# Two bottleneck blocks on one core: the step from the first 1x1 convolution into the 3x3 one, with ScalarE's order written out, idle matmuls moved, and a product split around another

## The chip, the cores and the metric

One core of one Trainium2 chip. The metric is the device time of one execution in microseconds; times in the profile are from the start of the profiled span. Engines are named as the profile names them: PE is TensorE's matmuls, PEld its weight loads, DVE is VectorE, ACT is ScalarE, POOL is GpSimd, SP is SyncE, which issues most transfers.

## What is computed

```python
def block(x, w1, b1, g1, be1, w2, b2, g2, be2, w3, b3, g3, be3, residual_scale):
    out = relu(bn(conv1x1(x, w1) + b1, g1, be1))        # 1024 -> 256 channels
    out = relu(bn(conv3x3(out, w2, pad=1) + b2, g2, be2))
    out = bn(conv1x1(out, w3) + b3, g3, be3)            # 256 -> 1024 channels
    return relu(x + softplus(residual_scale)[0] * out)

x = block(x, *first_weights)       # x: 64 x 1024 x 14 x 14, float32
x = block(x, *second_weights)
```

`bn` normalises each channel by the mean and the variance of the whole batch, so a convolution has to be finished before its result can be normalised.

## The kernel before

**Stages.** Block one's first 1x1 convolution runs by itself (up to about 305 us). Its 3x3 convolution follows (to 584 us), then statistics of the third convolution by way of a Gram matrix, then a fused stage in which block one's last convolution and block two's first one alternate (to 1259 us), then block two's 3x3 convolution (to 1541 us), its Gram matrix and its last convolution. The activations between the convolutions, 256 channels in two halves ("slots"), stay in SBUF as `y`.

**The 1x1 convolutions** are block products with 7 instead of 8 products (class `Seven`). Product k is the method `pk`; each of the first convolution's has CS // 2 = 4 matmuls on one PSUM bank, and the methods are generators that yield after each matmul. p6, p7 and p4 add to the same bank `y`; after p7, `after7` has ScalarE copy that bank out (`saved`), before p4 adds to it. The last tiles of images go through `Conv1.closing`, which writes the order of the products out: p1, p4 of the tiles before, p6, p5, p7, p4, then `border.affine_of(1)` and `border.norm(1)` (scale, shift and normalisation of slot 1), and the rest. `late` is true in block one, where a tile pair has 392 columns a matmul, and false in block two, where it has 196.

**The 3x3 convolution** (`conv2`) is Winograd-like. Rows go in six linear combinations per group of 8 images (8 groups, NG), made by VectorE: the pairs (1, 2), (3, 4) and (5, 0). For each combination i VectorE makes `r`, and from it `sums`, `diffs` and `v` (differences of neighbouring columns); ScalarE fills in the two edge columns of `v` (lines 682 and 683). TensorE makes products: `m` from `sums`, `l` from `diffs`, and `columns` from `v`, added to a bank pair on which ScalarE has first put `m` (`put`, lines 835 and 837). ScalarE copies `l` to `ls` (`middle`, lines 849 and 851), and VectorE adds `columns` and `ls` to `f` (line 870), from which the rows of the result are put together in `finish`. Bank pairs `columns`, banks `l` and banks `m` are double.

**The border.** The first pair of combinations is made slot by slot (`first_combination`), slot 1 ahead, begun within `closing` by `border.steps`. Its two products, `first` and `second`, are done in parts by slot: the loop over `s` at the end of `conv2`. In that loop `first` adds `m` straight to its bank pair, and between two steps two matmuls of 448 columns by the identity run on `second.banks`; what they leave there is overwritten by `second.put`. After the loop, the products follow each other in a fixed pattern: `item.middle`, `item.columns(EVEN)`, the next product's `start` (its `m` and `put`), `item.columns(ODD)`, `finished.send(item)`.

**What sets the order.** A scheduling layer orders each engine's instructions. Those that go through `tc.keep_in_program_order` (all matmuls by the helper at line 175, ScalarE's by the helper `act` at line 338, VectorE's by `run`) keep the program's order on their engine; the others are placed by the layer. So a bare `nc.scalar.activation` may come before or after its neighbours in the program.

Of the kernel before, what the change touches and what calls it, by code (L numbers as in the profile page):

```python
# [42 lines left out]
P = 128  # L43
# [47 lines left out]
def bottlenecks(ctx: ExitStack, tc: tile.TileContext, x, w1s, w2s, w3s, pars, out):  # L91
# [248 lines left out]
    class Conv1(Seven):  # L340
# [41 lines left out]
        def closing(self, before):  # L382

            border = self.border
            late = len(self.ts) > 1

            def summary(s):
                summarize(self.stats[:, s : s + 1], T // 2 - 1, T - len(self.ts), PX)  # L390

            yield from self.p1()
            yield from before.p4()
            summary(1)
            if not late:
                yield from before.p3()
                summary(0)
            yield from self.p6()
            yield from self.p5()
            yield from self.p7()  # L400
            yield from self.p4()
            border.affine_of(1)
            border.norm(1)
            if late:
                yield from before.p3()
                summary(0)
            border.begin()
            if late:
                border.steps(1)
            yield from self.p2()  # L410
            if late:
                border.steps(2)
            yield from self.p3()
            border.affine_of(0, lambda: border.steps(1 if late else 3))
            border.norm(0)
            border.steps(5 if late else 6)
# [181 lines left out]
    def conv2(b, par, aff, early, rest):  # L598
# [50 lines left out]
        class Inputs:  # L649

            def __init__(self, pair, run=lambda ins: None):
                self.pair, self.run = pair, run
                self.tiles = tiles = full if pair[0] == 3 else RT
                self.lines = lines = tiles * GI
                n = len(pair) * MS * lines

                def part(tag, width):
                    v = place(tag, 2 * MS * RT * GI * width)  # L660
                    return v[:, : n * width].rearrange("p (k s l c) -> p k s l c", k=2, s=MS, c=width)

                self.r, self.v = part("r", W), part("v", W)
                self.sums, self.diffs = part("sums", WH), part("diffs", WH)
# [8 lines left out]
            def step_columns(self, k=slice(0, 2), s=both):  # L673
# [8 lines left out]
                nc.scalar.activation(v[:, :, :, :, 0], r[:, :, :, :, 0], AF.Copy)  # L682
                nc.scalar.activation(v[:, :, :, :, W - 1], r[:, :, :, :, W - 1], AF.Copy, scale=-1.0)

            def subtract_columns(self, k=slice(0, 2), s=both):
                r = self.r[:, k, s]
# [26 lines left out]
        def first_combination(x, s, t):  # L713

            run, here = x.run, slice(s, s + 1)
            ra, rb = (x.rows(k)[:, s] for k in range(2))
            t = t.rearrange("p (r l) -> p r l", r=RT)
            t2, t1 = t[:, :, :LINE], t[:, :, LINE:]  # L720
            act(t[:, RT - 1], y_all[:, s, GPX - 2 * LINE : GPX], AF.Copy, scale=-3.0)
            run(stt(t[:, :full], two_rows(0, s)[:, :, 0], -4.0, two_rows(0, s)[:, :, 1]))
            yield
            run(nc.vector.tensor_add(ra, t1, t2))
            yield
            x.add_columns(slice(0, 1), here)
            yield
            first, second = x.subtract_columns, x.step_columns
            if s == 0:
                first, second = second, first  # L730
            first(slice(0, 1), here)
            yield
            second(slice(0, 1), here)
            yield
            run(nc.vector.tensor_sub(rb, t1, t2))
            yield
            x.add_columns(slice(1, 2), here)
            yield
            x.subtract_columns(slice(1, 2), here)
            yield  # L740
            x.step_columns(slice(1, 2), here)
            yield

        def combine(g, pair):
            x = Inputs(pair)
            ra, rb = (x.rows(k) for k in range(2))

            if pair[0] == 1:
# [39 lines left out]
        class Products:  # L788
# [39 lines left out]
            def put(self, m):  # L828

                if True:  # L830
                    for q in (EVEN, ODD):
                        v = self.banks[:, q]
                        if self.i == 1:
                            for o in range(MS):
                                nc.scalar.activation(v[:, o], m[:, o], AF.Identity, bias=par[:, B2 + o : B2 + o + 1])
                        else:
                            nc.scalar.activation(v, m, AF.Copy)  # L837

            def middle(self, l=None):

                if l is None:
                    l = self.whole("l", DIFF, self.diffs)
# [2 lines left out]
                for q, sign in (EVEN, 1.0), (ODD, -1.0):  # L845
                    if self.first:
                        for o in range(MS):
                            bias = par[:, B2 + o : B2 + o + 1]
                            nc.scalar.activation(self.ls[:, q, o], l[:, o], AF.Identity, bias=bias, scale=sign)
                    else:  # L850
                        nc.scalar.activation(self.ls[:, q], l, AF.Copy, scale=sign)

            def columns(self, *qs, slots=range(MS), sums=None):
                steps = {ODD: (D3M1, self.r[:, :, :, WH:]), EVEN: (D0M2, self.r[:, :, :, :WH])}
# [171 lines left out]

        inputs = Inputs(order[0], tc.keep_in_program_order)
        t = early.tile([P, RT * 2 * LINE], FP, tag="fa", name="t")  # L1030
        yield from first_combination(inputs, 1, t)
        psum, pool, stats = rest
# [7 lines left out]
            pass  # L1040
        coming, finished = items(), finish()
        next(finished)
        queue.append(next(coming))

        both_columns = EVEN, ODD
        first.open()
        second.open()
        l, m, l2 = first.bank("l"), second.bank("m"), second.bank("l")
        for s in reversed(range(MS)):
            first.columns(*both_columns, slots=[s], sums=True)  # L1050
            if s:
# [658 lines left out]
```

## Time and profile before

| | |
|---|---|
| median of 3 runs | 1929.17 us (1928.47 to 1929.77) |
| profiled execution | 1928.93 us |
| its span | 1927.2 us |
| TensorE (PE) busy | 1905.0 us |
| VectorE (DVE) busy | 1547.5 us |
| ScalarE (ACT) busy | 1085.5 us |
| mean granted TensorE clock | 0.997 of full speed |

A row of the timeline has the start, the length, the engine, the line of the source, the operation, the tiles (output, arrow, inputs), shapes and the number of instructions merged into the row; the brackets hold the engine's idle time before the row and what ended it. A matmul of four-byte numbers stands as two records, so four matmuls are "x8". The ends of matmuls are modelled, some 0.16 us later than the start of the next one in a running stream. A row of waits has the sum in microseconds, the count and the longest one.

### The profile page before, as it was taken

What the parts mean: (1) busy time and instruction counts of PE and PEld (TensorE: products, weight loads), DVE (VectorE), ACT (ScalarE), POOL (GpSimd) and SP (SyncE); (2) the same over time, 40 slices, a digit from 0 to 9 for tenths busy, and PEclk for the clock granted to TensorE, in tenths of its full rate; (3) what the DMA queues carried; (4) which work ended last, traced back from release to release, by engine and by line L of the source; (5) the groups of instructions that cost most, each with busy time, mean ns of one, the idle gap of its engine ahead of it and who ended that gap; (6) DMA issues with size and microseconds to landing.
All of it is one profiled execution on the core that took longest, in us unless ns stands there. A gap on an engine that the chain in (4) does not pass through costs nothing.

```text
span 1927.2 us, 28719 instructions
## 1 busy us (share of the span) xinstructions
PE 1905.0 (99%) x10232; PEld 1600.9 (83%) x10232; DVE 1547.5 (80%) x2509; ACT 1085.5 (56%) x2152; POOL 565.2 (29%) x678
## 2 busy tenths in 40 slices
PE   9999998999999999999999999989999999999999
PEld 5555557999998899999999999989999986555555
DVE  5788767999998866676767767789999986888886
ACT  2222214677778355555555555546777682666666
POOL 0111100211204143433434334302121041666664
PEclk9999999999999999999999999999999999999999
DMA  7777634797856544444444444348879466889998
GB/s 287 273 249 276 220 148 134 202 228 207 213 180 169 190 162 169 168 171 180 179 173 168 167 180 179 123 151 208 221 207 224 141 170 236 291 326 348 329 336 301
DMA packets 198527, 408.77 MB, mean 212 GB/s; under 512 B 37104, under 2 KB 175024, under 8 KB 181872
## 3 DMA queue, kind: packets, MB, share of 16 engines
q1 hardware_dynamic: 159712, 321.85, 49.0%
q0 software_dynamic: 33056, 34.03, 8.5%
q10 hardware_dynamic: 5616, 51.06, 6.4%
q8 instruction: 81, 1.33, 0.3%
q14 instruction: 62, 0.51, 0.1%
HBM read 263.75 MB, written 115.34 MB: 197 GB/s over the span
## 4 chain that ended last, share of the span: by engine, by line
PE 95%; DVE 2%; DMA 1%; ACT 1%; issue 1%; POOL 0%; SPq 0%; DVEq 0%; ACTq 0%; POOLq 0%
PE ay L175 18%; PE cy L175 17%; PE columns L175 14%; PE cp L175 12%; PE ap L175 10%; PE m L175 7%; PE l L175 7%; PE cx L175 5%; PE ax L175 5%; PE ps L175 1%; DMA x<-mid 0%; DMA home<-y 0%; DMA x<-in_x 0%; POOL home L1160 0%; DVE v L677 0%
## 5 line engine op out<-in xcount | busy, mean ns | idle before, releaser
L338 ACT ACTIVATE cu<-cy,scale 128x196 f32<-128x196 f32 (+1 forms) x552 | 256.7, 474 | 278.4 <-PE cy L175 273.2
L175 PE MATMUL columns<-v,ub 128*128 128x224 f32 (+1 forms) x1536 | 303.7, 339 | 5.7 <-ACT columns L837 5.7
L338 ACT ACTIVATE x<-x,shift 128x392 f32<-128x392 f32 x452 | 255.0, 613 | 72.6 <-POOL x L534 53.5
L175 PEld LDWEIGHTS columns<-v,ub 128*128 128x128 f32 x1536 | 270.0, 189 | 11.1 <-ACT columns L837 6.4
L508 DVE SCALAR_TENSOR_TENSOR x<-cp,scale,x 128x196 f32<-128x196 f32 (+1 forms) x368 | 177.8, 483 | 98.6 <-PE cp L175 96.9
L175 PE MATMUL cy<-ct,ws 128*128 128x196 f32 (+1 forms) x736 | 221.8, 383 | 1.2 <-ACT cu L338 1.2
L175 PE MATMUL ay<-at,ws 128*128 128x196 f32 (+1 forms) x768 | 212.7, 382 | 0.0
L529 POOL TENSOR_TENSOR x<-x,cu 128x196 f32<-128x196 f32 (+1 forms) x184 | 159.8, 869 | 171.9 <-ACT cu L338 163.9
L534 POOL TENSOR_TENSOR x<-x,cu 128x392 f32<-128x392 f32 x124 | 125.9, 1016 | 191.4 <-DVE x L508 191.4
L175 PEld LDWEIGHTS ay<-at,ws 128*128 128x128 f32 x768 | 139.3, 190 | 34.5
L175 PEld LDWEIGHTS cy<-ct,ws 128*128 128x128 f32 x736 | 133.4, 190 | 36.4 <-ACT cu L338 4.2
L175 PE MATMUL l<-diffs,ub 128*128 128x224 f32 (+1 forms) x768 | 150.4, 338 | 1.0 <-PE columns L175 0.6
L555 POOL TENSOR_TENSOR x<-x,cu 128x392 f32<-128x392 f32 x120 | 121.9, 1017 | 86.3 <-DVE x L508 81.5
L175 PE MATMUL m<-sums,ua 128*128 128x224 f32 (+1 forms) x752 | 146.3, 337 | 0.2 <-DVE sums L671 0.2
L338 ACT ACTIVATE au<-ay 128x196 f32<-128x196 f32 (+1 forms) x140 | 53.5, 382 | 150.8 <-PE ay L175 148.1
L175 PEld LDWEIGHTS l<-diffs,ub 128*128 128x128 f32 x768 | 134.9, 190 | 2.9 <-PE columns L175 1.2
L508 DVE SCALAR_TENSOR_TENSOR x<-cx,scale,x 128x196 f32<-128x196 f32 (+1 forms) x184 | 89.0, 484 | 56.8 <-PE cx L175 56.8
L175 PEld LDWEIGHTS m<-sums,ua 128*128 128x128 f32 x752 | 132.1, 190 | 1.2 <-DVE sums L671 0.5
L175 PE MATMUL cy<-y,w 128*128 128x196 f32 (+1 forms) x408 | 125.3, 393 | 0.0
L175 PE MATMUL cx<-y,w 128*128 128x196 f32 (+1 forms) x400 | 122.6, 391 | 0.0
L837 ACT ACTIVATE columns<-m 128x448 f32<-128x448 f32 (+1 forms) x160 | 78.6, 491 | 70.5 <-PE m L175 68.3
L175 PE MATMUL cp<-y,ws 128*128 128x196 f32 (+1 forms) x368 | 113.6, 390 | 0.6 <-DVE x L508 0.6
(234 smaller groups left out, 3949.6 us busy)
## 6 DMA issues: line engine op xcount, KB each, us to landing
x<-in_x SPq DMA_DIRECT2D x62, 1568.0 KB, 7.0
ub<-u SPq DMA_DIRECT2D x92, 768.0 KB, 5.7
x<-mid SPq DMA_DIRECT2D x32, 1568.0 KB, 8.3
mid<-x ACTq DMA_DIRECT2D x31, 1568.0 KB, 5.1
out<-x SPq DMA_DIRECT2D x123, 392.0 KB, 5.2
ua<-u SPq DMA_DIRECT2D x92, 256.0 KB, 3.3
u<-y POOLq DMA_DIRECT2D x48, 256.0 KB, 5.7
home<-y SPq DMA_DIRECT2D x70, 96.0 KB, 3.6
```

Of the source, the lines that this page charges most:

```text
L175: tc.keep_in_program_order(nc.tensor.matmul(*args, **kw))
L338: tc.keep_in_program_order(nc.scalar.activation(*args, **kw))
L508: nc.vector.scalar_tensor_tensor(v, bank, self.scale[:, o : o + 1], v, ALU.mult, ALU.add)
L529: nc.gpsimd.tensor_add(self.part(1, 1), self.part(1, 1), u3)
L534: nc.gpsimd.tensor_add(v, v, self.u12)
L555: nc.gpsimd.tensor_add(v, v, self.u12[:, i * self.n : (i + 1) * self.n])
L837: nc.scalar.activation(v, m, AF.Copy)
```

## The change

- `closing`: two of the four matmuls of another product (p3 of the tiles before in block one, p2 in block two) are issued between p7 and p4; the other two follow `border.norm(1)`.
- `Inputs`: the two edge copies of ScalarE become a method, `step_edges`. `first_combination` calls it right after the first row sum, ahead of VectorE's other steps (in both slots). They and the edge copies of pair (3, 4) of group 0 are issued by `act`, in the program's order.
- The border loop: `second.put` and `second.middle` and the bias form of `middle` are issued by `act`; `second.middle` moves up to the end of the loop, ahead of `finished.send(first)`. The next pair's combination, `next(coming)`, moves from before the loop to after `second.middle`.
- Idle matmuls: `fill`. In block one they stay where they were (two). In block two four are issued ahead of the loop, and none in it.

In the order of instructions that the scheduling layer makes of it, TensorE changes by these alone, and GpSimd's and SyncE's queues keep their order. On ScalarE, around the border, the two edge copies of pair (3, 4) move from before the first `ls` (block one) or from between the bank copies (block two) to after the second product's `ls`; in block two the third product's bank copies then come ahead of the four row copies into `r`, in block one they stay behind them. On VectorE, block one is the same up to the second group's combination, where an `f` moves ahead of `sums` and `diffs` moves behind the writes of `y`, just ahead of the next `steps`; in block two `f` of the first product moves ahead of `sums` of pair (3, 4), `f` of the second ahead of the second step into `r`, and a few later ones change places up to the second group.

```diff
@@ closing
             yield from self.p7()
+
+            between = before.p3() if late else self.p2()
+            yield from itertools.islice(between, CS // 4)
             yield from self.p4()
             border.affine_of(1)
             border.norm(1)
+            yield from between
             if late:
-                yield from before.p3()
                 summary(0)
             border.begin()
             if late:
                 border.steps(1)
-            yield from self.p2()
+                yield from self.p2()
...
@@ Inputs
-            def __init__(self, pair, run=lambda ins: None):
-                self.pair, self.run = pair, run
+            def __init__(self, pair, run=lambda ins: None, copy=nc.scalar.activation):
+                self.pair, self.run, self.copy = pair, run, copy
...
+            def step_edges(self, k=slice(0, 2), s=both):
+
+                r, v = self.r[:, k, s], self.v[:, k, s]
+                self.copy(v[:, :, :, :, 0], r[:, :, :, :, 0], AF.Copy)
+                self.copy(v[:, :, :, :, W - 1], r[:, :, :, :, W - 1], AF.Copy, scale=-1.0)
+
+            def step_columns(self, k=slice(0, 2), s=both, edges=True):
+                if edges:
+                    self.step_edges(k, s)
...
@@ first_combination
             run(nc.vector.tensor_add(ra, t1, t2))
+            x.step_edges(slice(0, 1), here)
             yield
             x.add_columns(slice(0, 1), here)
             yield
-            first, second = x.subtract_columns, x.step_columns
+            first, second = x.subtract_columns, partial(x.step_columns, edges=False)
...
@@ combine
-            x = Inputs(pair)
+            x = Inputs(pair, copy=act if g == 0 and pair[0] == 3 else nc.scalar.activation)
...
@@ Products
+            def fill(self, times=1):
+
+                n = MS * self.n
+                for q in (EVEN, ODD) * times:
+                    v = self.banks[:, q].rearrange("p o n -> p (o n)")
+                    matmul(v, ident, ident[:, :1].to_broadcast([P, n]), start=True, stop=True)
+
+            def put(self, m, copy=nc.scalar.activation):
...
-                            nc.scalar.activation(v, m, AF.Copy)
+                        copy(v, m, AF.Copy)
...
-                            nc.scalar.activation(self.ls[:, q, o], l[:, o], AF.Identity, bias=bias, scale=sign)
+                            act(self.ls[:, q, o], l[:, o], AF.Identity, bias=bias, scale=sign)
                     else:
-                        nc.scalar.activation(self.ls[:, q], l, AF.Copy, scale=sign)
+                        copy(self.ls[:, q], l, AF.Copy, scale=sign)
...
@@ the border at the end of conv2
-        inputs = Inputs(order[0], tc.keep_in_program_order)
+        inputs = Inputs(order[0], tc.keep_in_program_order, act)
...
-        queue.append(next(coming))
...
         l, m, l2 = first.bank("l"), second.bank("m"), second.bank("l")
+        if b == 1:
+            second.fill(2)
         for s in reversed(range(MS)):
             first.columns(*both_columns, slots=[s], sums=True)
             if s:
                 first.part(l, DIFF, first.diffs, s)
-                n = MS * second.n
-                for q in both_columns:
-                    v = second.banks[:, q].rearrange("p o n -> p (o n)")
-                    matmul(v, ident, ident[:, :1].to_broadcast([P, n]), start=True, stop=True)
+                if b == 0:
+                    second.fill()
             first.columns(*both_columns, slots=[s])
             if s == 0:
                 first.part(l, DIFF, first.diffs, s)
                 first.middle(l)
             second.part(m, SUM, second.sums, s)
             if s == 0:
-                second.put(m)
-                long_work(0, 0)
-                finished.send(first)
+                second.put(m, act)
             second.part(l2, DIFF, second.diffs, s)
+        second.middle(l2, act)
+        queue += list(itertools.islice(coming, 1))
+        long_work(0, 0)
+        finished.send(first)
         queue = queue[1:] + list(itertools.islice(coming, 1))
         for k in range(1, NG * NF):
             item, more = queue[0], queue[1:2]
             qs = both_columns
-            item.middle(l2 if k == 1 else None)
+            if k > 1:
+                item.middle()
```

More of the change, by code (lines that the diff above doesn't have):

```diff
@@ L671, in add_columns @@
                 self.run(nc.vector.tensor_add(self.sums[:, k, s], r[:, :, :, :, WH:], r[:, :, :, :, :WH]))
-            def step_columns(self, k=slice(0, 2), s=both):
+            def step_edges(self, k=slice(0, 2), s=both):
[5 more added lines that the diff above has]
+                    self.step_edges(k, s)
                 r, v = self.r[:, k, s], self.v[:, k, s]
@@ L681, in step_columns @@
                 )
-                nc.scalar.activation(v[:, :, :, :, 0], r[:, :, :, :, 0], AF.Copy)
-                nc.scalar.activation(v[:, :, :, :, W - 1], r[:, :, :, :, W - 1], AF.Copy, scale=-1.0)
             def subtract_columns(self, k=slice(0, 2), s=both):
@@ L826, in open, with middle @@
                 self.banks = columns()[:, :, : MS * self.n].rearrange("p q (o n) -> p q o n", o=MS)
[L828 to L839, printed above, removed]
+            def fill(self, times=1):
[4 more added lines that the diff above has]
+            def put(self, m, copy=nc.scalar.activation):
+                for q in (EVEN, ODD):
+                    v = self.banks[:, q]
+                    if self.i == 1:
+                        for o in range(MS):
+                            nc.scalar.activation(v[:, o], m[:, o], AF.Identity, bias=par[:, B2 + o : B2 + o + 1])
+                    else:
+                        copy(v, m, AF.Copy)
+            def middle(self, l=None, copy=nc.scalar.activation):
                 if l is None:
```

## The prediction

> **What bounds the kernel now.** I read the page's engine totals first, then who waited for whom on TensorE, then the stretches around the longest waits, then the timelines of TensorE, ScalarE and VectorE there.
>
> ```profile
> PE 1905.0 (99%) x10232; PEld 1600.9 (83%) x10232; DVE 1547.5 (80%) x2509; ACT 1085.5 (56%) x2152; POOL 565.2 (29%) x678
> ...
> PE columns L175 <- ACT columns L837: 5.7, 2, 4.5
> PE columns L175 <- issue: 3.8, 1, 3.8
> ...
> PE ay L175 <- ACT au L338: 1.0, 2, 0.6
> ```
>
> TensorE is the bound: its waits come to some 17 us, and the first two lines (sum, count, longest) hold 9.5 of them. All three lines lie at the two borders, about 287 to 330 us (block one) and 1250 to 1290 us (block two). Columns of the next view: stretch, length, busy time and count of PE, weight loads, DVE, ACT and POOL, granted clock, DMA share, GB/s.
>
> ```profile
> 320.00:325.00 5.00, 2.48 (x7) 2.28 (x8) 4.66 (x6) 4.34 (x12) 0.00 (x0) 0.78 0.30 100
> 1260.00:1265.00 5.00, 1.77 (x5) 1.66 (x6) 4.66 (x16) 2.96 (x6) 0.15 (x2) 0.65 0.86 263
> 1265.00:1270.00 5.00, 5.00 (x16) 3.85 (x15) 4.79 (x11) 1.94 (x8) 0.00 (x0) 0.67 0.33 122
> ```
>
> The long waits are paid twice: the clock is below 1 after them. TensorE's timeline, block one and then two:
>
> ```profile
> 317.12 0.92 PE L175 MATMUL l<-diffs,ub 128*128 128x224 f32 x4
> 322.52 3.09 PE L175 MATMUL columns<-v,ub 128*128 128x224 f32 x8 [4.48 <-ACT columns L837]
> ...
> 1263.23 3.33 PE L175 MATMUL columns<-sums,ua 128*128 128x224 f32 x8 [3.81 <-issue]
> 1266.35 1.70 PE L175 MATMUL l<-diffs,ub 128*128 128x224 f32 x4
> 1267.84 1.92 PE L175 MATMUL columns<-ident 128*128 128x448 f32 x4
> 1269.59 1.70 PE L175 MATMUL columns<-v,ub 128*128 128x224 f32 x8
> ...
> 1279.33 1.81 PE L175 MATMUL columns<-v,ub 128*128 128x224 f32 x8 [1.19 <-ACT columns L837]
> ```
>
> Eight records of 224 columns take 3.1 us after either long wait, and 1.55 elsewhere. What held ScalarE in block one:
>
> ```profile
> 319.16 0.37 ACT L682 ACTIVATE v<-r 128x96 f32<-128x96 f32 x1 [5.39 <-DVE r L640]
> 319.44 0.35 ACT L683 ACTIVATE v<-r 128x96 f32<-128x96 f32 x1
> 319.69 1.45 ACT L849 ACTIVATE ls<-l,par 128x224 f32<-128x224 f32 x4
> ...
> 321.90 0.57 ACT L837 ACTIVATE columns<-m 128x448 f32<-128x448 f32 x1
> ```
>
> The edge copies of the next pair stood first in ScalarE's order and waited 5.39 us for VectorE, while l had been ready since 316.5; the bank copy that TensorE needs came last.
>
> [...] waits of 4.48 and 3.81 us are followed by half rate, the one of 1.19 us is not. [...] That is the third wait above: product four adds to the bank that ScalarE is copying out (0.59 us at 294.17, 0.42 at 1255.17).
>
> **Part one, two matmuls ahead of product four.** A product takes 2.63 us in block one (eight records), so two of its four matmuls take 1.32. Without its wait product four could start at 293.42 (294.17 less 0.59, less the 0.16 of modelled tail). It will start at 293.42+1.32=294.74, not at 294.17; the row after a wait costs 0.1 more (2.73 from start to start), which is saved, so it ends 0.47 late. On it hang, one after the other, y, its statistics, the scale, the norm, VectorE's first sums (304.44) and the first columns (304.89): 0.47 late, with TensorE idle from about 304.1, some 1.5 us. The next wait, for diffs at 307.15, hangs on VectorE's step at 305.00, which today waits 0.17 for TensorE; so from there on 0.3 late. In block two the half product takes 0.665: 1254.59+0.67=1255.26 against 1255.17, and the saved 0.1 cancels it: nothing lost. TensorE is through with the convolution at 1258.6 instead of 1259.3. Split product and whole one write the same results; nothing else moves on VectorE, and the DMA queues keep their order. The weight loads that wait for the freed activations start no later.
>
> **Part two, idle matmuls in block two.** Two of 448 columns took 1.52 us at full clock (307.98 to 309.50); four take 3.04, from 1258.6 to 1261.6. They write a bank whose users are already done; the one wait before them is on TensorE itself. VectorE's sums (1262.73+0.39) are unmoved, so TensorE then idles 1.6 us, well under the 3.81 that halved the clock. I take full clock: first columns 1.51 instead of 3.12, l 0.76 instead of 1.49, the two old idle matmuls (1.75) gone: 4.1 us. The next v is ready at 1264.74, before it is needed at 1265.5, and later inputs are just in time (sums 1268.39, needed 1268.55). Below: none if the clock is half all the same (bounds of this part, 1.75 and 4.1).
>
> **Part three, ScalarE's order.** In the new order the four ls, the two bank copies and the next two ls come first, the edge copies after.
> Block one: l is out at 316.53+0.3; four ls 1.33, two bank copies 1.03, hand-over 0.1: TensorE goes on at 319.3, not 322.52: 3.2. The wait shrinks to 1.1, so the half rate (4.44 us for 2.68 of work) goes too: 1.8. Sum 5.0. What is late next: the third product's bank copies stand behind four row copies (1.41 us) that wait for VectorE's diffs, which now end at 319.5 plus sums 0.78, v 1.27, f 1.00, diffs 0.85, 323.4. So 323.4+1.41+0.90=325.7, while TensorE has reached it at 324.7: 1.0 back. Those columns begin at 325.7 instead of 329.64: **3.9**.
> Block two: l out at 1272.5, plus 1.33 and 1.03: TensorE at 1275.0 instead of 1279.33, 4.3. Then f is ahead of sums on VectorE (1.0 us): sums end at 1277.3 while TensorE is there at 1276.6. The third m begins at 1277.3, not 1280.97: **3.7**.
>
> **What VectorE gives back.** It is busy 33 of 34 us in each group of the convolution (32.8 to 33.7 in windows of 34), so it cannot follow freely. Block two: from the second product's f (1283.26 was the start of that run, with no idle until the diffs end at 1305.68) 22.4 us of work remain; f can now start at 1280.2, when TensorE has the second columns out, so diffs end at 1302.6 and TensorE's l starts 3.1 early instead of 3.7. **Block two: 3.1.**
> Block one: VectorE advances only 1.4 (its idle at 328.70). In its new order diffs stand after the five writes of y, just before the step at 348.31: they end at 348.31-1.4=346.9, and TensorE comes at 350.29-3.9=346.4: 0.5 lost, 0.6 with the restart. In the next group ScalarE's copy of fa (400.01) stands between the two bank copies, and TensorE had 0.7 to spare there (400.74 to 401.46). With TensorE 3.2 and VectorE 1.8 ahead, 0.7 is lost; I put 0.8 for that group. **Block one: 3.9-0.6-0.8=2.5.** Later groups keep their order, and TensorE's lead over VectorE is used up.
>
> **The sum.** 3.1+2.5=5.6 us. What follows the convolutions waits on TensorE's and VectorE's last products, including the loads of x, so it moves along. The profiled execution took 1928.93 us (span 1927.2, 1.7 around it): 1923.3. It is 0.24 under the median of 1929.17, so as a median **1923.6 us**.
>
> **Rivals.**
> - VectorE takes all that it can: TensorE keeps 1.4 and 3.1, 4.5: 1924.7. For it: 0.3 to 1.0 us of idle per group. Against: TensorE reads most of its operands over 3 us after they are made (sums 354.96 for m at 359.44).
> - Nothing is given back: 3.9+3.7=7.6: 1921.6. It needs VectorE's diffs earlier than its order has them.
> - The clock still halves, in the 1.5 and 1.6 us waits ahead of the first columns. Price as in the rows: 1.8 and 2.3. At one border 1925.5 or so, at both 1927.7. Against: 1.19 us left it alone.
> - Slower: VectorE becomes the bound of both convolutions. ScalarE serves TensorE's copies earlier and its row copies for VectorE later (VectorE waits 0.6 for them once a group), VectorE loses that again in each group, and its slack is gone. At twice the wait, 0.6 more in 14 groups is 8.4: 1932.0 after the gain of 5.6. It decides from 0.4 a group. Against: from the second group on the order is the old one.
> - That the change misses its mark: the idle matmuls could wait for the readers of the old bank (until 1260.0); then they end at 1263.1 and part two is the same.
>
> **Numbers.** Forecast 0.57 (its own range 1922.3 to 1924.6), VectorE takes all 0.20, nothing given back 0.10, clock 0.10, slower 0.03. Range 1921.2 to 1925.8: the outer gains, less or more than the spread of the runs (0.7), and the clock at one border. About 0.2%, 3.9 us, is what a measurement can tell from no change: faster by more than that means under 1925.3, the forecast, the third case and most of the first rival: 0.80; same 0.17; slower 0.03.
>
> **What would show it.** Clock 1.00 in both borders; TensorE on second columns near 319.3 and 1275.0 with waits of about 1.1; four idle matmuls ahead of the first columns of block two; first columns of block one about 0.5 late; waits of TensorE on l behind diffs near 347 and 1302.6. It is wrong if the clock falls, if TensorE waits for VectorE in every group, or if a wait behind the row copies at 325 is over 2 us.

## The result, and the profile after

The changed kernel takes **1924.15 us** (median of 11 runs, 1922.67 to 1927.3); the kernel before took 1928.66 us in its 11 runs of the same session (1927.42 to 1930.24). The ratio is 0.9975, with a 95% interval of 0.9965 to 0.9984: 3.1 to 6.8 us less. The profiled execution took 1924.15 us, its span 1922.4 us, 4.8 less than before. The forecast was 1923.6 us.

The page's engine line and TensorE's waits (sum, times, longest) after the change:

```profile
PE 1903.6 (99%) x10236; PEld 1598.7 (83%) x10236; DVE 1547.8 (81%) x2509; ACT 1085.1 (56%) x2152; POOL 566.0 (29%) x678
```

```profile
PE columns L175 <- ACT columns L338: 2.1, 2, 1.0
PE l L175 <- PE columns L175: 1.8, 3, 0.8
...
PE columns L175 <- issue: 1.5, 1, 1.5
...
PE columns L175 <- DVE sums L674: 1.2, 1, 1.2
```

The waits of 4.5 and 3.8 us are gone, and so are the two of product four on ScalarE's copy of its bank. In their place stand several of about 1 us; those on `l` (second line) and on `sums` (last line) are behind VectorE. The view puts the waits on `l` down to PE, but in the timelines the `l` of the second group starts 0.1 us after VectorE's `diffs` has ended, in both blocks. TensorE has four matmul records more than before, the two more idle matmuls, and is busy 1.4 us less: the half rate is gone. The stretches at the borders, columns as before:

```profile
320.00:325.00 5.00, 4.63 (x29) 4.32 (x27) 4.60 (x5) 2.23 (x8) 0.00 (x0) 1.00 0.50 148
1260.00:1265.00 5.00, 4.05 (x21) 4.04 (x22) 4.79 (x14) 2.68 (x6) 0.00 (x0) 1.00 0.76 259
1265.00:1270.00 5.00, 5.00 (x28) 4.94 (x28) 4.86 (x9) 0.82 (x4) 0.00 (x0) 1.00 0.12 34
```

The granted clock (third number from the end) is 1.00 where it was 0.78, 0.65 and 0.67. TensorE's timeline, first block one, then block two:

```profile
305.08 1.78 PE L175 MATMUL columns<-sums,ua 128*128 128x224 f32 x8 [1.25 <-DVE sums L674]
...
319.00 1.81 PE L175 MATMUL columns<-v,ub 128*128 128x224 f32 x8 [1.03 <-ACT columns L338]
...
325.36 1.42 PE L175 MATMUL columns<-v,ub 128*128 128x168 f32 x8 [0.72 <-ACT columns L853]
...
346.88 1.75 PE L175 MATMUL l<-diffs,ub 128*128 128x224 f32 x8 [0.62 <-PE columns L175]
...
1256.31 3.18 PE L175 MATMUL columns<-ident 128*128 128x448 f32 x8
1260.95 1.75 PE L175 MATMUL columns<-sums,ua 128*128 128x224 f32 x8 [1.46 <-issue]
...
1272.88 1.81 PE L175 MATMUL columns<-v,ub 128*128 128x224 f32 x8 [1.04 <-ACT columns L338]
...
1300.56 1.75 PE L175 MATMUL l<-diffs,ub 128*128 128x224 f32 x8 [0.78 <-PE columns L175]
```

What released ScalarE, in block one:

```profile
316.50 1.46 ACT L338 ACTIVATE ls<-l,par 128x224 f32<-128x224 f32 x4 [2.79 <-PE l L175]
317.83 1.12 ACT L338 ACTIVATE columns<-m 128x448 f32<-128x448 f32 x2
318.87 0.97 ACT L338 ACTIVATE ls<-l 128x448 f32<-128x448 f32 x2
319.71 0.64 ACT L338 ACTIVATE v<-r 128x96 f32<-128x96 f32 x2
323.09 0.39 ACT L640 ACTIVATE r<-y 128x224 f32<-128x224 f32 x1 [2.74 <-DVE diffs L696]
```

Now the `ls` wait for TensorE's `l` and start with it, the bank copies follow, and the edge copies stand behind.

**Where the time came from.** I compare stretches, not the whole span. Block one's stretch runs from the start of product six (the row `ay<-at,ws` at 285.52 before, 285.23 after) to the first matmul `m<-ident` behind the convolution. Block two's runs from the row `ap<-x,ws` near 1249, where TensorE waits 0.3 us for `y`, to the first `m<-ident` behind its convolution. Block one takes 298.55 us before and 296.22 after, block two 291.51 and 288.60: 2.33 and 2.91 us less. These two lengths are the better measure: block two takes 288.58 to 288.60 us in the changed kernel and in the four runs below that leave its idle matmuls there and VectorE's order in block two alone, and block one takes 296.22 us both here and in the run that leaves it untouched. The rest of the program is not so steady: over all fourteen profiles the part ahead of block one's stretch takes 285.1 to 286.7 us, the part between the two 665.0 to 666.2, and the part behind 384.5 to 387.7, in no order that follows an edit.

TensorE's lead over the kernel before, from the start of each row in both timelines (0.29 us, by which the changed kernel's profile entered block one earlier, taken off; in block two 2.28):

| TensorE starts | before | after | lead | forecast |
|---|---|---|---|---|
| block one, first columns | 304.89 | 305.08 | -0.5 | -0.47 |
| l behind diffs | 307.15 | 307.09 | -0.2 | -0.3 |
| second columns | 322.52 | 319.00 | 3.2 | 3.2 |
| l, after the half clock | 328.50 | 323.33 | 4.9 | 5.0 |
| third columns | 329.64 | 325.36 | 4.0 | 3.9 |
| l of the second group | 350.29 | 346.88 | 3.1 | 3.3 |
| end of the stretch | 584.07 | 581.46 | 2.3 | 2.5 |
| block two, first columns | 1263.23 | 1260.95 | 0.0 | 0 |
| next v | 1269.59 | 1263.30 | 4.0 | 4.1 |
| second columns | 1279.33 | 1272.88 | 4.2 | 4.3 |
| l of the second group | 1305.77 | 1300.56 | 2.9 | 3.1 |
| end of the stretch | 1540.71 | 1535.52 | 2.9 | 3.1 |

### The profile page after: what moved, and what is told of

Read it like the earlier page. It is cut to its first block, busy times and chain, and to the rows that moved or that the text cites. A ratio compares the mean times of both kernels' runs of the same rounds, so it can differ in the third digit from the quotient of the medians.

```text
span 1922.4 us, 28731 instructions
## 1 busy us (share of the span) xinstructions
PE 1903.6 (99%) x10236; PEld 1598.7 (83%) x10236; DVE 1547.8 (81%) x2509; ACT 1085.1 (56%) x2152; POOL 566.0 (29%) x678
## 4 chain that ended last, share of the span: by engine, by line
PE 93%; DVE 4%; DMA 2%; issue 1%; ACT 1%; POOL 0%; SPq 0%; DVEq 0%; ACTq 0%; POOLq 0%
PE ay L175 17%; PE cy L175 17%; PE columns L175 13%; PE cp L175 11%; PE ap L175 10%; PE m L175 7%; PE l L175 6%; PE cx L175 5%; PE ax L175 4%; PE ps L175 1%; DMA x<-mid 1%; DMA home<-y 1%; DVE v L688 0%; DMA out<-x 0%; DVE steps L773 0%
## 5 line engine op out<-in xcount | busy, mean ns | idle before, releaser
L175 PE MATMUL cy<-ct,w 128*128 128x196 f32 (+1 forms) x368 | 110.9, 383 | 0.5 <-ACT cu L338 0.5
```

The costliest lines, as they stand in the source:

```text
L175: tc.keep_in_program_order(nc.tensor.matmul(*args, **kw))
```

## The experiments

**Theory.** Block one's gain is ScalarE's order, block two's the idle matmuls, which leave the loop and take the place of idleness ahead of the first columns; the split costs a little. TensorE is then ahead of VectorE by more than VectorE's order allows, and what is over is waited for at `l`. **Rivals:** the split brings part of the gain; a wait taken from TensorE is kept in full; the row copies on ScalarE, not VectorE, are what comes next.

All lengths below are of the two stretches; "before" for the times is the kernel before in the same session, 1929.23 us for the first four; 1928.82 for the one with the bank copies first and the one without idle matmuls; 1929.15 for the other four.

The scheduling layer answers some of these edits by moving instructions of VectorE and ScalarE too. By the profiles, both engines keep the order of the kernel that was edited, instruction by instruction, in the run without the split, in block one of the run with ScalarE's order alone, and in every block that an edit leaves untouched. Where they do not, the text says so.

### One part alone, three times

The split alone, on the kernel before:

```diff
             yield from self.p7()
+            between = before.p3() if late else self.p2()
+            yield from itertools.islice(between, CS // 4)
             yield from self.p4()
...
+            yield from between
```

> The kernel before with the split product alone. Measured as the time from the start of p6 in the closing order to the first filler matmul behind the 3x3 convolution: 298.55 us in block one before and 296.23 in the changed kernel; in block two, from the first p6 matmul after its short wait, 291.51 and 288.60. Theory (the gain is ScalarE's order in block one and the idle matmuls in block two; the split puts product four later and so costs): block one 0.2 to 0.4 slower than before, the 4.5 us wait and the half clock still there. Rival (the split gives what it covers, 0.6 and 0.4): block one 0.6 faster. Block two is not clean: the scheduling layer places ScalarE's and VectorE's steps there differently from before, so up to 2 us faster may come of that alone.

1926.83 us, ratio 0.9988 (0.998 to 0.9996). Block one 299.61, block two 290.20. Block one has the new wait of 1.25 us and keeps the old one of 4.48. It is 1.06 us longer than in the first profile of the kernel before, more than expected; the last two runs show that the clock accounts for all but 0.20 of it. In block two the wait ahead of the first columns is 4.48 instead of 3.81, as the half product is through earlier, and the half rate follows it (3.32 us for the eight records of these columns, 1.75 in the changed kernel); yet the stretch is 1.3 us shorter, and the later waits at `m` and `l` are gone. The run isn't clean there: with this edit the scheduling layer also put VectorE's and ScalarE's free instructions in another order, and which of these moves shortened it stays open. Block two is judged by the fourth run instead.

The idle matmuls of block two alone, on the kernel before (`fill` is a function in the border there):

```diff
+        if b == 1:
+            fill(2)
         for s in reversed(range(MS)):
...
-                for q in both_columns:
-                    v = second.banks[:, q].rearrange("p o n -> p (o n)")
-                    matmul(v, ident, ident[:, :1].to_broadcast([P, n]), start=True, stop=True)
+                if b == 0:
+                    fill(1)
```

> The kernel before with the idle matmuls of block two moved alone (four ahead of the first columns, none in between); ScalarE's calls and the product order are those of before. Theory (VectorE sets what TensorE keeps in block two, so ScalarE's order adds nothing there): block one unchanged, block two 2.7 to 3.0 of the 2.9 us that the whole change gains there; total 1.5 per mille, some 1925.8. Rival (parts add up; ScalarE's order and the split bring 1 us or more of block two): block two 1.5 to 2.0.

1926.65 us, ratio 0.9987 (0.9979 to 0.9995). Block two 288.67: 2.84 of the 2.91 us, at clock 1.00. It is not the idle matmuls entirely alone: with this edit the scheduling layer gave VectorE in block two the changed kernel's order exactly, and ScalarE too but for one `ls`. What that order does without the idle matmuls, the next run shows. Block one, whose instructions are those of before, took 299.39 instead of 298.55; the last two runs deal with that.

ScalarE's order alone (and the few changes of place on VectorE that come with it): the changed kernel with the product whole and the idle matmuls back in the loop in both blocks:

```diff
-            between = before.p3() if late else self.p2()
-            yield from itertools.islice(between, CS // 4)
             yield from self.p4()
...
-        if b == 1:
-            second.fill(2)
...
-                if b == 0:
-                    second.fill()
+                second.fill()
```

> The changed kernel without the split product and with the idle matmuls of block two back between the steps: ScalarE's written order alone. Theory: block one gains all that the change gains and the 0.3 that the split costs, 2.6; block two keeps its 3.8 us wait and the half clock and gains 0.5 to 1.0. Rival (the split and the rest add up): block one 1.7, block two 0.2 or less.

1925.58 us, ratio 0.9983 (0.9976 to 0.999). Block one 296.02: 2.53 us less than before, more than the whole change brings there. Block two 291.14: 0.37 less, under the 0.5 to 1.0 expected. VectorE has the changed kernel's order there but for one exchange, of the first `f` and `sums`; on ScalarE two of the row copies come earlier. TensorE's timeline of this run:

```profile
1260.49 3.33 PE L175 MATMUL columns<-sums,ua 128*128 128x224 f32 x8 [3.82 <-issue]
```

The old wait and the half rate after it are still there. So the order by itself, VectorE's included, is worth little in block two, and the idle matmuls almost all: with them, in the next run, it is 288.60. The parts don't add: the three single gains in time, 2.4, 2.6 and 3.7 us, come to more than the whole, and `l` of the second group in block one waits 0.61 us here as it waits 0.62 with the whole change.

### The split taken out

The changed kernel, with p3 or p2 as a whole behind `norm(1)` again:

```diff
-            between = before.p3() if late else self.p2()
-            yield from itertools.islice(between, CS // 4)
             yield from self.p4()
```

> The changed kernel with the products whole again, nothing else; ScalarE's and VectorE's orders are the same instruction by instruction. Theory: block one 0.3 faster than the changed kernel (gain 2.6 to 2.7), first columns 0.2 to 0.45 earlier; block two the same (2.9), with a wait of 0.42 at product four and a shorter one after the idle matmuls. Rival (the split gives what it covers): block one 0.6 and block two 0.4 slower than the changed kernel.

1923.47 us, ratio 0.9973 (0.9963 to 0.9984). Block one 296.02, 0.20 us shorter than with the split; block two 288.60, the same. TensorE waits for the bank, and then not at the first columns:

```profile
295.38 2.90 PE L175 MATMUL ay<-at,w 128*128 128x392 f32 x8 [0.59 <-ACT au L338]
...
306.11 1.78 PE L175 MATMUL columns<-sums,ua 128*128 128x224 f32 x8
```

The split removes a wait of 0.59 us and makes one of 1.25 on what hangs on product four. In block two the wait of 0.42 us comes back, and the one ahead of the first columns goes from 1.46 to 0.79. All other orders being the same, the split brings nothing in either block; that rival is out.

### What takes the gain back

The changed kernel with four idle matmuls ahead of the loop in both blocks, and none in it:

```diff
-        if b == 1:
-            second.fill(2)
+        second.fill(2)
...
-                if b == 0:
-                    second.fill()
```

> The changed kernel with block one treated as block two: its four idle matmuls stand ahead of the first columns, and the two inside the loop are gone. Theory (VectorE is next in line and takes back most of what TensorE is spared): the waits of 1.25 us ahead of the first columns and 0.23 at l near 307 go, clock 1.00, but the waits on v near 319 and 325 and on diffs near 346.9 stay at about 1.0, 0.8 and 0.7, and block one is 0.3 to 0.5 us shorter than in the changed kernel: about 1923.8 against 1924.15. Rival (a wait removed from TensorE is time saved): both waits are kept as a gain, 1.5 us: about 1922.7. Block two is the same under both.

1923.66 us, ratio 0.9972 (0.996 to 0.9983). Both waits at the first columns and at `l` near 307 are gone, 1.48 us; block one is 295.80, 0.42 us shorter. The waits of 1.03 and 0.80 us on `v` and 0.71 on `diffs` stand. As the theory had it, though the 0.42 us is not of the idle matmuls alone: the scheduling layer also moved some of VectorE's and ScalarE's instructions in block one, the second group's `v` to behind the writes of `y`.

The changed kernel without two of VectorE's writes of `y`, one row of the result in both halves of the channels, in block one's first group (0.8 us together):

```diff
-                        stt(out_rows[1][:, o, :full], e[:, o], 2.0, d3[:, o])
+                        if g or b:
+                            stt(out_rows[1][:, o, :full], e[:, o], 2.0, d3[:, o])
```

> The changed kernel with two of VectorE's writes left out: those of the second output row of the first group of block one (two instructions, about 0.9 us together), so that these rows of y are not the reference's in block one. Theory (the wait of 0.62 us at l near 346.9 is VectorE's queue that is behind): the wait on diffs there goes, and block one is 0.4 to 0.6 us shorter: about 1923.7. Rival (the distance between diffs and l is fixed by ScalarE's and TensorE's own order, and VectorE's volume has no part in it): the wait at l stays 0.6 and the time 1924.15. Block two is the same under both.

1922.64 us, ratio 0.9969 (0.9956 to 0.9981). Block one 295.64, 0.58 us shorter. TensorE's `l` of the second group:

```profile
346.87 1.75 PE L175 MATMUL l<-diffs,ub 128*128 128x224 f32 x8
```

No wait is left on that row. TensorE's order is the same, and the row starts 0.37 us earlier in the stretch, as VectorE's `diffs` ends 0.36 earlier: it is VectorE's queue that stood behind it. The 0.58 us is not of the two writes alone: five small instructions of VectorE's statistics came forward with this edit (the `l` near 307 waits 0.50 us for it instead of 0.23), and a few others changed places.

The changed kernel with `diffs` ahead of `v` on VectorE, in every group:

```diff
-            x.step_columns()
             x.subtract_columns()
+            x.step_columns()
```

> The changed kernel with the two steps of VectorE between products exchanged: the subtraction that gives diffs ahead of the additions that give v. Theory (what took the gain back is that diffs stands behind v in VectorE's queue): the waits of 0.62 and 0.78 us at l near 346.9 and 1300.6 go; v comes about 1 us later, which shows as a wait of 0.5 to 1.3 us on v further on in block one and as none in block two; block one 0.4 us shorter, block two 1.4: about 1922.4. Rival (VectorE's volume is what counts and its order only moves the wait from l to the columns on v): the waits come back under v in both blocks with the same sum, 1924.1.

1921.8 us, ratio 0.9963 (0.995 to 0.9977). Block one 295.62 (0.60 shorter than the changed kernel), block two 287.10 (1.50). The changed kernel's VectorE in block two, then this one's:

```profile
1297.71 1.75 DVE L688 TENSOR_TENSOR v<-r 128x1536 f32<-128x1536 f32 x1
1299.38 1.08 DVE L696 TENSOR_TENSOR diffs<-r 128x896 f32<-128x896 f32 x1
```

```profile
1298.12 1.08 DVE L696 TENSOR_TENSOR diffs<-r 128x896 f32<-128x896 f32 x1
1299.12 1.75 DVE L688 TENSOR_TENSOR v<-r 128x1536 f32<-128x1536 f32 x1
```

TensorE, in this run:

```profile
1300.04 1.68 PE L175 MATMUL l<-diffs,ub 128*128 128x224 f32 x8
1301.55 1.70 PE L175 MATMUL columns<-v,ub 128*128 128x224 f32 x8
```

TensorE needs `diffs` before `v`; VectorE made them the other way round. With the same work on VectorE (1547.0 us busy against 1547.8), the waits of 0.78 and 0.62 us are gone, and so is the one of 0.72 at the third columns. In block one the second group's `diffs` comes ahead of the writes of `y` this way, 7.3 us earlier in the stretch, and `v` behind them; 0.39 and 0.90 us come back there as waits on `v` at 354.56 and 383.21, in block two none. That VectorE's amount of work set the end is refuted for block two.

The changed kernel with the third product's bank copies and, in group 0, all four row copies issued by `act`, so that the bank copies come first:

```diff
-                nc.scalar.activation(rb[:, :, 0], y_grp[:, :, g, 1], AF.Copy, scale=-1.0)
+                copy = act if g == 0 else nc.scalar.activation
+                copy(rb[:, :, 0], y_grp[:, :, g, 1], AF.Copy, scale=-1.0)
...
-                v.start()
+                v.start(act if k == 1 else nc.scalar.activation)
```

> The changed kernel with ScalarE's bank copies of the third product ahead of its row copies in the first group of both blocks, which is what the prediction priced at 1.0 us for block one. Theory (VectorE sets the next time in any case): the wait of 0.72 us on v near 325 goes, but the one on diffs near 346.9 grows from 0.62 to about 1.1, and block one is 0.2 to 0.5 us shorter than in the changed kernel: 1923.8 against 1924.15. Rival (the copies' 1.0 us is on the path that sets the end): 0.8 to 1.0 us shorter, 1923.2. Block two is the same under both.

1923.26 us, ratio 0.9973 (0.9961 to 0.9984). Block one 296.10: 0.12 us shorter, less than either expected. The timeline of TensorE:

```profile
324.62 1.32 PE L175 MATMUL columns<-v,ub 128*128 128x168 f32 x8
...
346.51 1.75 PE L175 MATMUL l<-diffs,ub 128*128 128x224 f32 x8 [1.09 <-issue]
```

The wait of 0.72 us is gone from the first row, and the second row waits 0.47 longer than the 0.62 it had; waits of 0.18 and 0.39 us at 377 and 381 are new. VectorE's order in block one changed with it; still the second row starts 0.1 us after `diffs` has ended, as without the edit. The row copies were in front of TensorE, but not in front of the end: that rival is out.

### The idle matmuls left out

The changed kernel, block two without any idle matmul:

```diff
-        if b == 1:
-            second.fill(2)
```

> The changed kernel without any idle matmul in block two. TensorE then has nothing for about 4.6 us ahead of the first columns (the 1.46 us that it waits now, and the 3.04 that the four idle matmuls fill), longer than the 3.81 after which the clock of the kernel before fell to half. Theory: the clock falls to about half for 3 to 4 us and costs TensorE about 1.7 us there, but the waits of 0.37, 0.78, 0.19 and 0.39 us behind it (VectorE's) become smaller by most of that: block two 0.2 to 0.6 us longer than in the changed kernel, 1924.5 against 1924.15. Rival one (the lost clock counts in full): block two 1.7 us longer, 1925.9. Rival two (the clock does not need the idle matmuls): clock 1.00 and block two the same. Block one is the same under all.

These matmuls are also the only ones with `start=True` on the second product's banks, and with them left out the result is off by 0.089 (relative); all other instructions are the same in number and shape. 1922.94 us, ratio 0.997 (0.9961 to 0.998): by the times it can't be told from the changed kernel. By the stretch it can: 289.52 us, 0.92 longer, between the theory's 0.2 to 0.6 and rival one's 1.7.

```profile
1260.00:1265.00 5.00, 4.67 (x13) 4.26 (x14) 4.76 (x14) 2.52 (x6) 0.00 (x0) 0.50 0.64 219
```

The clock fell to half during a wait of 4.48 us (from 1255 to 1260 it is 0.87). TensorE's second columns came 2.57 us later than in the changed kernel (28.53 us into the stretch against 25.96), its `l` of the second group 1.34, the end 0.92: the loss at the border was larger than the 1.7 expected, and two thirds of it was made up later, where TensorE had waited for VectorE in any case (0.18 us at that `l`, not 0.78). Rival two is out. How much was made up is rough, as the orders of VectorE and ScalarE in block two changed with the edit.

Against the run with ScalarE's order alone, whose two idle matmuls stand in the loop (block two 291.14), this one is 1.62 us shorter, although its clock was at half for longer (6.83 us against 3.42). So of the 2.54 us that moving the idle matmuls brought, the larger part came of their leaving the loop, and some 0.9 of the clock that they keep up ahead of it.

### All that the runs pointed to

The changed kernel with four of these edits together: the product whole, four idle matmuls ahead of the loop in both blocks, the bank copies ahead of the row copies, and `diffs` ahead of `v`:

```diff
-            between = before.p3() if late else self.p2()
-            yield from itertools.islice(between, CS // 4)
...
-        if b == 1:
-            second.fill(2)
+        second.fill(2)
...
-                v.start()
+                v.start(act if k == 1 else nc.scalar.activation)
...
-            x.step_columns()
             x.subtract_columns()
+            x.step_columns()
```

> The changed kernel without the split of the product, with the idle matmuls ahead of the first columns in both blocks, with the third product's bank copies ahead of the row copies on ScalarE, and with diffs ahead of v on VectorE. Theory: the waits at the first columns, on v near 325 and on diffs near 346.9 and 1300.6 are all gone, one of about 1.1 us on v near 319 and one at 1275 are left; block one 1.8 us shorter than in the changed kernel and block two 1.4, of which the last stage and the Gram part give back 0.3 to 0.6: about 1921.4. Rival (the steady part of the convolutions is VectorE's, so that what the borders gain is waited for later): each block gains at most 0.5: 1923.2.

1920.7 us (1919.49 to 1921.76), ratio 0.9957 (0.9945 to 0.997), the fastest of the study. Block one 294.67, 1.55 us shorter than the changed kernel, block two 287.11, 1.49. The row after the border in block one:

```profile
319.48 1.81 PE L175 MATMUL columns<-v,ub 128*128 128x224 f32 x8 [1.03 <-ACT columns L338]
```

Behind it one wait of over 0.1 us is left on TensorE in the whole convolution, 0.18 us at 376.48. Bank copies ahead of the row copies were worth 0.12 us by themselves; with `diffs` early, the four parts together bring 1.55 (1.8 were expected, and 1.4 in block two), more than the singly measured 0.20, 0.42, 0.12 and 0.60, which add up to 1.34.

### The kernel before, twice more

> The kernel before, unchanged, profiled again. In the runs that left block one as it was, the 4.5 us wait was followed by a half-clock stretch that cost 3.4 us of clock, against 1.7 in the first profile of the kernel before, and block one was 0.84 to 1.06 us longer with it. Theory (where the fall of the clock lies against the wait differs from execution to execution): block one, from the sixth product to the first matmul of the Gram part, lies anywhere from 298.5 to 299.6 us with the kernel unchanged, in step with the clock lost between 320 and 330 us. Rival (those edits lengthened block one): 298.5 to 298.6 again.

> The same kernel once more, with the same expectations: under the theory block one lies between 298.5 and 299.6 us, under the rival it is 298.5 to 298.6 in both.

Nothing is edited. One execution each: 1931.64 and 1930.57 us; another one in the same session took 1927.63, at a mean clock of 0.998. Block one 299.63 and 299.66, just above the expected range, block two 291.94 and 291.98. Timeline of TensorE in the second of them:

```profile
322.54 3.35 PE L175 MATMUL columns<-v,ub 128*128 128x224 f32 x8 [4.48 <-ACT columns L837]
325.69 2.44 PE L175 MATMUL m<-sums,ua 128*128 128x168 f32 x8
327.93 1.84 PE L175 MATMUL columns<-v,ub 128*128 128x224 f32 x8
```

and its stretches:

```profile
320.00:325.00 5.00, 2.46 (x7) 2.23 (x8) 4.65 (x6) 4.37 (x12) 0.00 (x0) 0.64 0.32 105
325.00:330.00 5.00, 5.00 (x22) 4.88 (x21) 2.42 (x4) 1.79 (x3) 0.00 (x0) 0.68 0.07 21
```

The same kernel, the same wait, and from the columns at 322.54 to the next `l` 7.07 us pass (329.61), where the first profile has 5.98. One minus the clock, times the length, gives 3.4 us of lost clock here and 1.7 in the first profile. Views that begin and end where the clock changes, first profile and then this one:

```profile
322.83:326.24 3.41, 3.41 (x11) 3.14 (x10) 2.93 (x4) 1.51 (x5) 0.00 (x0) 0.50 0.00 0
321.38:328.20 6.82, 5.66 (x17) 5.35 (x18) 5.51 (x6) 3.02 (x9) 0.00 (x0) 0.50 0.02 6
```

The clock is at half for 3.41 us in one and 6.82 in the other, and TensorE (first busy time) works for 3.41 and 5.66 us of that. At half the clock the work takes about twice its time: block two's first columns, from their start to that of the next row, took 3.12 us in the first profile, at clock 0.50, and 1.59 in the changed kernel, at 1.00. So half of that work is taken as the loss:

| run | clock at half | TensorE at work in it | block one | less half of that work |
|---|---|---|---|---|
| before, first profile | 322.83 to 326.24 | 3.41 | 298.55 | 296.84 |
| before, second | 321.46 to 328.29 | 5.63 | 299.63 | 296.82 |
| before, third | 321.38 to 328.20 | 5.66 | 299.66 | 296.83 |
| idle matmuls alone | 320.58 to 327.41 | 5.12 | 299.39 | 296.83 |
| split alone | 321.05 to 327.88 | 5.16 | 299.61 | 297.03 |

The theory held: the clock accounts for the whole difference. The idle matmuls of block two did not lengthen block one, and the split costs 0.20 us there, as in the changed kernel. The record has the mean granted clock of 64 more executions of the kernel before, in three sessions: 27 at 0.996, as in these two profiles, 15 at 0.997, as in the first, and 22 at 0.998 or above, with medians of 1930.01, 1928.75 and 1928.19 us. The first profile was a middling one, then, and these two were dear ones.

## Why the prediction was right, step by step

**The mechanism and the sizes held.** Forecast and result differ by 0.55 us, and the spread of the runs is larger. By the median alone the forecast could not be told from the first rival (1924.7), since 1924.15 lies halfway; the stretches tell them apart: that rival had block one keep 1.4 us, and it kept 2.33.

- *Part one.* The first columns came 0.48 late (0.47 worked out), `l` 0.23 late (0.3). At the end of the stretch it is 0.20, by the run with the whole product. In block two nothing, as said. A slip changed nothing: from 304.1 to 305.36 TensorE idles 1.26 us, not 1.5 (1.25 measured).
- *Part two.* 4.1 us predicted, 4.0 read at the next `v`; the wait left was 1.46 (1.6), the clock full. That the clock halves is refuted for waits of 1.25 and 1.46 us as they lay here. The part's lower bound, 1.75 with the clock at half, is near the 1.62 of the run without idle matmuls.
- *Part three.* 3.2, 5.0 and 3.9 us in block one: 3.2, 4.9, 4.0. In block two 4.3 and 3.7: 4.2 and 3.6. The terms are not sums to be kept, though: the 1.0 us behind the row copies was right where it stood, and removing it brought 0.12.
- *What VectorE gives back.* Block one 0.6 and 0.8: 0.9 and 0.8. Block two 0.6: 0.7. So the two blocks came to 5.2 us (2.33 and 2.91), not 5.6. This step was right on the place and nearly on the size, and half right on the cause: "it cannot follow freely" because it is busy 33 of 34 us. The exchange of two instructions in each group, with no work taken away, gave 0.60 and 1.50 us. VectorE's order was the cap first, its amount only behind that.
- *"It moves along."* What follows the convolutions was to keep the gain. In the two first profiles the part between gave back 0.3 and the last one 0.4, and block one was entered 0.29 earlier. Those are within what the same parts vary by in other profiles, so no loss is shown, and none of this size is excluded.
- *The size of "before".* All steps were taken from one profile, whose half clock in block one was 1.1 us cheaper than in two others. That this profile lay near the middle of the executions was luck, as one profile cannot show it. Against those two, the stretches are 3.4 and 3.4 us shorter. Of the interval of the ratio, 3.1 to 6.8 us, the sum of the first comparison (5.2) lies inside and that of the second (6.8) at its edge, as it should be if some executions are of either kind.

Slower by VectorE in each group: no such waits came. Behind the `l` of the second group TensorE's waits of over 0.1 us come to 0.20 us in block one and 0.58 in block two.

## What to carry to other kernels

An engine's wait is worth what the next engine in line lets through: here 4.9 and 4.2 us on TensorE became 2.3 and 2.9, and the cheap next step was to let VectorE make first what TensorE reads first. If idle matmuls are to be had, put them where the engine has nothing to do anyway: two of them took 1.75 us inside the loop, and four ahead of it filled idle time and kept the clock at 1.00, where it was 0.50 without them. After an edit, compare the order of every engine's instructions, not only that of the one that was edited. Where whole runs differ by more than the change, measure stretches between fixed points of the trace, and profile the kernel before more than once.

## What the runs showed of the hardware

The price of a long wait varied with nothing changed: after the same 4.48 us, 1.7 or 3.4 us of clock were lost, and block one was 1.1 us longer. The traces show what differed. At the borders the clock is at half eleven times in these fourteen profiles, twice for 3.41 us and nine times for 6.83. The stretch was the short one where TensorE was back at work before the fall (at 322.52, the fall at 322.83, in block one of the first profile) or 0.04 us after it, and the long one where it came back 0.88 us or more after it (at 322.54, the fall at 321.38, in block one of the third). What sets the moment of the fall was not shown.

So a long wait has no fixed price here. Nor does the clock of block two fall at the end of the 3.81 us: in the first profile it fell at 1261.49, 2.1 us after TensorE's last matmul had ended at 1259.42 and 1.7 before the next one began at 1263.23:

```profile
1258.08:1261.49 3.41, 1.34 (x9) 1.03 (x7) 3.06 (x14) 2.38 (x4) 0.15 (x2) 1.00 0.42 101
1261.49:1268.32 6.83, 5.09 (x13) 4.54 (x14) 6.43 (x18) 3.07 (x9) 0.00 (x0) 0.50 0.75 257
```

The 1.46 us that are left there now lost no clock in any of the five profiles that have them; what a wait longer than these and shorter than 3.81 does there, no run shows. I had priced the half clock as a fixed 1.8 us, from one profile.
